# A planned kernel of four graph layers: a longer time in the plan for the transfers that sum the scores

## The chip, the cores and the metric

The kernel runs on one core of one Trainium2 chip. The metric is the device time of one execution in microseconds (us). Before the change it is 1678.89 us, the median of three runs (1675.96 to 1679.08).

A core has four engines that compute: TensorE (PE in the profile; PEld is its loading of weights), VectorE (DVE), ScalarE (ACT) and GpSimd (POOL). SyncE (SP) issues most of the transfers. Each engine takes its own instructions in the order in which the program lists them, and waits at an instruction until what it needs is there.

## What is computed

The input is 32 graphs of 512 nodes with 128 features each, and one adjacency matrix of 512 x 512 for all of them. Four layers follow each other; each normalises the features, applies a ReLU and adds its result to x. The change concerns layer 0, whose core is

```python
x_h = elu(h @ Wi + bi)
a_src = x_h @ We[:H, 0]
a_tgt = x_h @ We[H:, 0]
e = sigmoid(a_tgt[:, :, None] + a_src[:, None, :] + be[0])
e = e * (adj + ALPHA * (adj == 0))
agg = e @ x_h
self_part = x_h * sum(e, axis=-1)
recv = elu(concat(agg, self_part) @ Wn + bn)
out = concat(recv, x_h) @ Wm + bm
```

Layer 1 is a gated recurrent step, done five times, with two products by the adjacency in the reference (here both with the same matrix, so the kernel computes one). Layer 2 is one product by the adjacency and one by a weight. Layer 3 sums three powers of the adjacency.

## The kernel before

**Tiles.** One graph's features are a tile of 128 partitions x 512 elements, float32, 256 KB. Everything is done in such tiles: there are 36 of the kind `f` for features and scores, 4 of the kind `q` for float32r parts, 8 PSUM banks (`b`), 8 pieces of device memory (`m`) for tiles that are turned, and some small kinds. Float32r values are the short form[...]; a float32 tile is split in a high and a low part where the exact sum is wanted.

**The order of the work.** The kernel is written as a list of operations. Each has an engine, a time that the engine is taken (`us`), a due time, the values it reads and writes, and a `result`: the time from the end of its issue until its result can be used. A planner (class `Plan`, method `order`) goes through this list with a clock of its own: when an engine is free, it gives it the ready operation with the smallest due time, takes tiles as they come free by that clock, and writes the operations down. That sequence is the program. The figures `us` and `result` so decide only which instruction stands ahead of which in each engine's order, and which tile it gets[...]. The planner works in two stretches: the first 18 us of its clock, with small idle matmuls (L301) where TensorE has nothing to do, and the rest. The rest is planned twice, for an adjacency that float32r holds exactly and for one that it does not; these inputs take the first.

**The graphs.** The due times are set per graph: `begin(b)` for layer 0, 14 us apart for the first four graphs, then 56 us apart, and 30 us for the last four. Layer 1 follows 42 us after `begin` for graphs 0 to 3 and 112 us after it for most others. Several graphs are in different layers at once, so that TensorE has the products of one while the other engines work on another. Layers 0 to 2 are listed graph by graph, and layer 3 for four graphs together.

**Layer 0 around the change** (`layer0`). For each graph ScalarE (L620, tanh) and VectorE (L623) make four tiles of scores, `es[0]` to `es[3]`. They go two ways. TensorE multiplies them with the messages (L631) into the bank `pn`. And they are summed over all 512 source nodes: for graphs 0 and 1 by four products with ones; for the 30 others the four tiles are first added by transfers. SyncE copies `es[0]` to a tile `sums` (L641), and GpSimd issues three transfers, each of which adds one more tile to it (L644). Each writes the tile that the one before has written, so each waits for it. Then ScalarE rounds the sum to its high part (L648), VectorE makes the low part (L649), TensorE totals both over the partitions with a matrix of ones (L654), VectorE multiplies x_h by the total (L657), and TensorE adds that product with Wn (L442, helper `product`) to `pn`. An elu and the last product with Wm (L667) end the layer.

**Other names in the profile.** L442 is the helper of all float32 products (u3T, w4T, w3T, w5T and u5T are the weights of layer 1, Wi and Wn those of layer 0). L821 is layer 1's and 2's product by the adjacency, L902 and L911 are layer 3's, and L884 is layer 2's weight. L846, L447 and L853 are VectorE, ScalarE and VectorE of the gate between w4T and u5T. Lines L383 to L420 turn a tile by way of device memory, `m<-f` and `f<-m`. L479 is a small operation of GpSimd in each layernorm.

Of the kernel before, what the change touches and what calls it, by code (L numbers as in the profile page):

```python
# [41 lines left out]
class Plan:  # L42
# [16 lines left out]
    def op(self, eng, us, due, emit, reads=(), writes=(), two=None, keep=0, result=None,  # L59
           earliest=0.0):  # L60

        two = eng == "POOL" if two is None else two
        o = Op(eng, us, self.RESULT[eng] if result is None else result, emit, two, keep)
        o.earliest = earliest
        for v in reads:
            o.before.add(v.writer)
        for v in writes:  # L70
            o.before.update(v.readers)
            if v.writer:
                o.before.add(v.writer)
            elif v.kind and v.slot is None:
                o.takes.append(v)
        for v in reads:
            v.readers.append(o)
        for v in writes:
            v.writer, v.readers = o, []
        o.vals = [v.whole or v for v in dict.fromkeys([*reads, *writes])]  # L80
        for v in o.vals:
            v.left += 1
        for v in [*reads, *writes, *o.vals]:
            self.vals[v] = True
        o.before -= {o, None}
        o.due = max([due, *(b.due for b in o.before)])
        for b in o.before:
            b.after.append(o)
        self.ops.append(o)
# [124 lines left out]
def tile_four_graph_layers(  # L214
# [63 lines left out]
    def at(v):  # L278
        if v.tile is not None:
            return v.tile  # L280
        return places[v.kind][v.slot] if v.whole is None else at(v.whole)[:, v.part]
# [152 lines left out]
    def product(w, src, due, dst=None, start=True, stop=True, blocks=False):  # L434

        dst = dst or Val("b")
        def emit():
            to, of = at(dst), at(src)
            if blocks:
                to = to.rearrange("p (c q i) -> p q c i", c=NC, i=32)  # L440
                of = of.rearrange("p (q c i) -> p q c i", c=NC, i=32)
            nc.tensor.matmul(to, at(w), of, start=start, stop=stop)  # L442
        op("PE", T_MM, due, emit, [src, w], [dst])
        return dst
# [104 lines left out]
    def layer0(b, h, due):  # L549
# [85 lines left out]
        if b < 2:  # L635
            ps = Val("b")
            for jc in range(NC):
                product(ones, es[jc], d, ps, start=jc == 0, stop=jc == NC - 1)
        else:
            sums = [Val("f")]  # L640
            op("SP", T_DMA, d - 10, lambda: nc.sync.dma_start(at(sums[0]), at(es[0])),  # L641
               [es[0]], [sums[0]], result=2.6)
            for e in es[1:]:
                op("POOL", 1.0, d - 10, lambda e=e: nc.gpsimd.dma_start(  # L644
                    at(sums[0]), at(e), accum_op=ALU.add), [e, sums[0]], [sums[0]],
                   two=False, result=3.0)
            high, low, ps = Val("q"), Val("q"), Val("b")
            op("ACT", T_COPY, d, lambda: nc.scalar.copy(at(high), at(sums[0])), [sums[0]], [high])  # L648
            op("DVE", T_VEC, d, lambda: nc.vector.tensor_tensor(  # L649
                at(low), at(sums[0]), at(high).bitcast(F32), op=ALU.subtract),  # L650
                [sums[0], high], [low], two=True)
            def total():
                for n, part in enumerate((low, high)):
                    nc.tensor.matmul(at(ps), at(ones_r), at(part), start=n == 0, stop=n == 1)  # L654
            op("PE", 2 * T_PASS, d, total, [high, low, ones_r], [ps])
# [23 lines left out]
    def first_layer(b):  # L679
        h = layernorm(b, begin(b))  # L680
        layer0(b, h, begin(b))
# [316 lines left out]
```

## Time and profile before

| | us |
|---|---|
| median of three runs | 1678.89 |
| the profiled execution's own time | 1678.16 |
| its span, from the first instruction to the last | 1676.4 |
| TensorE busy | 1662.9 |
| VectorE busy | 1420.3 |
| ScalarE busy | 1130.5 |
| GpSimd busy | 239.6 |

The profile shows one execution. Busy time is the time in which an engine has an instruction under way; ends of matmuls are modelled, so that TensorE's busy time says little on whether it could be faster. "Idle before" is the time that an engine stood still just ahead of an instruction, with the one that released it. The clock granted to TensorE was full (0.999) throughout. The 90 adding transfers carry 23.6 MB in all and take 8.5% of the time of the 16 DMA engines; all others together take about a third.

### The profile page before, as it was taken

The page shows a single profiled execution, that of the slowest core. Times are in us where ns is not written, and L with a number is a line of the kernel's source. Part 1 is how long each engine was busy: PE and PEld are TensorE (multiplying, and loading weights), DVE is VectorE, ACT ScalarE, POOL GpSimd, SP SyncE. Part 2 cuts the span into 40 slices and gives each one's busy share as a digit, 9 for nine tenths or more (in the row PEclk, how much of TensorE's full clock was granted, in tenths as well). Part 3 has the DMA queues.
Part 4 walks back from the last instruction along what each step waited for, and adds up shares of the span by engine and source line. Part 5 has one row for each costly group of instructions (what it writes and reads, how often), then busy time and mean ns, then how long its engine had stood idle before and what let it go on. Part 6 is the DMA issues. An engine that isn't in the chain of part 4 may idle for free.

```text
span 1676.4 us, 21509 instructions
## 1 busy us (share of the span) xinstructions
PE 1662.9 (99%) x6615; PEld 1073.7 (64%) x6615; DVE 1420.3 (85%) x3327; ACT 1130.5 (67%) x2145; POOL 239.6 (14%) x243
## 2 busy tenths in 40 slices
PE   9999999999999999999999999999999999999998
PEld 7555555556666666666666666666666666666797
DVE  6888999999988888889888898888999988877742
ACT  8877677876875676656676676665777767655541
POOL 2311101211111111111101111111121110000110
PEclk9999999999999999999999999999999999999999
DMA  3444424444445434444434444344554543222301
GB/s 108 114 107 138 134 88 138 121 130 115 134 113 138 120 96 127 110 122 131 121 106 111 130 127 127 107 123 109 135 138 122 138 111 103 88 64 88 93 10 53
DMA packets 284157, 188.05 MB, mean 112 GB/s; under 512 B 77312, under 2 KB 236928, under 8 KB 284032
## 3 DMA queue, kind: packets, MB, share of 16 engines
q1 hardware_dynamic: 271072, 162.98, 32.5%
q0 software_dynamic: 12960, 23.60, 8.5%
q8 instruction: 54, 0.88, 0.2%
q14 instruction: 71, 0.58, 0.1%
HBM read 82.25 MB, written 72.81 MB: 92 GB/s over the span
## 4 chain that ended last, share of the span: by engine, by line
PE 62%; DMA 2%; DVE 1%; ACT 0%; issue 0%; SPq 0%; DVEq 0%; POOLq 0%
PE b L442 27%; PE b L821 13%; PE b L911 9%; PE b L902 5%; PE b L631 3%; PE b L667 2%; PE b L884 1%; DMA f<-f 1%; PE b L568 1%; DMA m<-f 1%; PE b L654 1%; DMA f<-m 0%; DVE f L383 0%; SPq L420 0%; ACT f L620 0%
## 5 line engine op out<-in xcount | busy, mean ns | idle before, releaser
L821 PE MATMUL b<-AQ,r 128*128 128x512 f32 x1024 | 303.8, 439 | 0.0
L431 ACT COPY f<-b 128x512 f32<-128x512 f32 x360 | 207.9, 586 | 120.6 <-PE b L821 87.2
L479 POOL TENSOR_TENSOR s<-s,nhalf 128x4 f32<-128x4 f32 x128 | 154.8, 1212 | 822.0 <-DVE s L477 702.6
L821 PEld LDWEIGHTS b<-AQ,r 128*128 128x128 f32 x1024 | 192.3, 188 | 89.3 <-issue 51.5
L846 DVE TENSOR_TENSOR f<-f,b 128x512 f32<-128x512 f32 x320 | 210.9, 676 | 26.6 <-PE b L442 26.2
L911 PE MATMUL b<-r,A_r 128*128 128x512 f32 x768 | 225.0, 427 | 0.0
L383 DVE STREAM_TRANSPOSE f<-f 128x512 f32<-128x512 f32 x244 | 204.7, 843 | 21.2 <-ACT f L487 20.4
L487 ACT ACTIVATE f<-x,s 128x128 f32<-128x128 f32 x512 | 210.5, 490 | 17.4 <-DVE s L482 16.9
L447 ACT ACTIVATE f<-f,b4w 128x512 f32<-128x512 f32 x160 | 115.4, 723 | 144.1 <-DVE f L846 143.5
L911 PEld LDWEIGHTS b<-r,A_r 128*128 128x128 f32 x768 | 139.0, 189 | 46.2 <-issue 24.4
L442 PE MATMUL b<-f,u5T 128*128 128x512 f32 x320 | 163.3, 593 | 1.0 <-DVE f L853 1.0
L442 PE MATMUL b<-f,u3T 128*128 128x512 f32 x320 | 163.3, 593 | 1.0 <-DMA f<-m 1.0
L442 PE MATMUL b<-f,w4T 128*128 128x512 f32 x320 | 162.8, 592 | 0.0
L442 PE MATMUL b<-f,w3T 128*128 128x512 f32 x320 | 162.4, 592 | 0.0
L442 PE MATMUL b<-f,w5T 128*128 128x512 f32 x320 | 162.4, 592 | 0.0
L644 POOL DMA_DIRECT2D f<-f x90 | 80.7, 896 | 536.4 <-DVE f L865 58.1
L821 PE MATMUL b<-A_r,r 128*128 128x512 f32 x512 | 151.9, 438 | 0.0
L863 DVE TENSOR_TENSOR f<-f,f 128x512 f32<-128x512 f32 x160 | 109.2, 683 | 48.9 <-ACT f L447 48.4
L902 PEld LDWEIGHTS b<-V,f 128*128 128x128 f32 x1024 | 131.4, 191 | 25.6 <-issue 19.9
L447 ACT ACTIVATE f<-b,b5w 128x512 f32<-128x512 f32 x160 | 109.4, 684 | 56.0 <-PE b L442 53.5
L447 ACT ACTIVATE f<-f,b3w 128x512 f32<-128x512 f32 x160 | 114.9, 719 | 43.1 <-DVE f L846 42.2
L795 DVE TENSOR_TENSOR r<-f,r 128x512 fp32r<-128x512 f32 x192 | 130.5, 682 | 12.6 <-ACT r L791 12.4
(106 smaller groups left out, 2539.3 us busy)
## 6 DMA issues: line engine op xcount, KB each, us to landing
m<-f SPq DMA_DIRECT2D x244, 256.0 KB, 2.1
f<-m SPq DMA_DIRECT2D x184, 256.0 KB, 2.9
f<-f POOLq DMA_DIRECT2D x90, 256.0 KB, 3.6
f<-m SPq DMA_DIRECT2D x240, 64.0 KB, 2.4
x<-in_x_dram SPq DMA_DIRECT2D x32, 256.0 KB, 3.2
out_dram<-x SPq DMA_DIRECT2D x32, 256.0 KB, 2.5
f<-f SPq DMA_DIRECT2D x30, 256.0 KB, 2.3
f<-d SPq DMA_DIRECT2D x28, 256.0 KB, 5.1
```

Of the source, the lines that this page charges most:

```text
L383: op("DVE", us, due, lambda: nc.vector.transpose(view_out(at(blocks)), view_in(at(src))), [src], [blocks])
L431: op("ACT", us, due, lambda: nc.scalar.copy(at(t), at(src)), [src], [t])
L442: nc.tensor.matmul(to, at(w), of, start=start, stop=stop)
L447: op("ACT", us, due, lambda: nc.scalar.activation(at(dst), at(src), AF.Tanh, bias=at(bias), scale=scale), [src, bias], [dst])
L479: op("POOL", 1.35, due, lambda: nc.gpsimd.tensor_tensor(stat(SCALE), stat(VAR), at(neg_half), op=ALU.pow), [s, neg_half], [s])
L487: nc.scalar.activation(at(h)[:, ts(c, P)], at(X[b])[:, c, :], AF.Relu, bias=stat(SHIFT)[:, c : c + 1], scale=stat(SCALE)[:, c : c + 1],)
L795: op("DVE", T_VEC, due, lambda: nc.vector.tensor_tensor(part(lo), whole(), part(hi).bitcast(F32), op=ALU.subtract), [src, hi], [lo], two=two)
L821: nc.tensor.matmul(at(pa), at(part)[:, ts(jc, P)], view(at(columns)[:, jc, :]), start=jc == n == 0, stop=jc == NC - 1 and n == PARTS - 1,)
L846: op("DVE", T_VEC, d, lambda: nc.vector.tensor_tensor(at(s), at(u), at(pg), op=ALU.add), [u, pg], [s])
L863: op("DVE", T_VEC, d, lambda c=c, h=h: nc.vector.tensor_tensor(at(c), at(c), at(h), op=ALU.subtract), [c, h], [c], two=True)
L902: nc.tensor.matmul(at(pz)[:, ts(i, D)], at(hT[i])[:, ts(ic, P)], at(V[k]), start=i == 0, stop=last and i == G - 1,)
L911: nc.tensor.matmul(at(pz), at(adjT)[:, jc, ts(ic, P)], at(part), start=False, stop=jc == NC - 1 and n == PARTS - 1,)
```

## The change

The planner's time from the end of the issue of an adding transfer to its result is longer; nothing else is touched.

```diff
             for e in es[1:]:
                 op("POOL", 1.0, d - 10, lambda e=e: nc.gpsimd.dma_start(
                     at(sums[0]), at(e), accum_op=ALU.add), [e, sums[0]], [sums[0]],
-                   two=False, result=3.0)
+                   two=False, result=4.6)
```

`op` takes the engine, the issue's time and the due time[...]. The planner now lists what depends on the sum, the next add first of all, as ready 1.6 us later after each add. The instructions are the same ones; their order and their tiles are the planner's.

## The prediction

> **What bounds the kernel now.** I read the page first, then the chain that ended last, then the waits, and last the timeline around the matmul that sums the scores.
>
> The page: the span, the engines, and the chain that ended last by engine.
>
> ```profile
> span 1676.4 us, 21509 instructions
> ...
> PE 1662.9 (99%) x6615; PEld 1073.7 (64%) x6615; DVE 1420.3 (85%) x3327; ACT 1130.5 (67%) x2145; POOL 239.6 (14%) x243
> ...
> PE 62%; DMA 2%; DVE 1%; ACT 0%; issue 0%; SPq 0%; DVEq 0%; POOLq 0%
> ```
>
> TensorE is busy nearly always, and what else is on the chain is small. But a busy TensorE may be a waiting one, so I take its true need from unbroken stretches of the chain (start us, duration us, what):
>
> ```profile
> 853.33 4.29 PE b L442 x10
> ...
> 1539.12 3.65 PE b L821 x16
> ...
> 1618.46 5.36 PE b L902 x48
> ```
>
> That is 0.429 us for each matmul of a float32 product, 0.228 for a float32r pass of 512 columns, 0.112 for one of 128 columns. By count: 2000 (L442, L631) x 0.429 = 858; 2368 float32r passes (L821, L911, L654, L809) x 0.228 = 540; 2154 narrow ones (L902, L667, L568, L884, the idle L301) x 0.112 = 241; 93 small ones about 9. Sum 1648 of the 1670 us until the last matmul ends; 6.4 us of subtractions and stores follow it. The 22 us between are: 1.0 before the first matmul, some 7 us spread over the float32r passes (0.231 instead of 0.228 apiece), and 13.4 us of true stalls, found as start-to-start intervals longer than the price of the matmul. No reordering can gain more than these 13.4 us, 0.8%. Whom TensorE waits for (us in total, times, longest), by recorded ends:
>
> ```profile
> PE b L654 <- DVE q L649: 2.8, 5, 0.9
> PE b L301 <- DVE ones L296: 1.0, 1, 1.0
> PE b L442 <- DVE f L853: 1.0, 2, 0.6
> PE b L442 <- DMA f<-m: 1.0, 1, 1.0
> PE b L631 <- DVE f L623: 0.6, 1, 0.6
> PE b L442 <- DVE f L657: 0.5, 2, 0.3
> ```
>
> The first is the matmul that totals the scores (L654); the last is the product right after it (Wn, behind L657). By start-to-start intervals L654 lost 3.7 us in 6 stalls, and 0.7 in the matmul behind it (after each stall the second matmul starts 0.1 late too); Wn 1.1 and 0.5. Together 6.0 us on the path to the total. The reason stands in the waits of the engines before it:
>
> ```profile
> ACT q L648 <- DMA f<-f: 29.9, 19, 4.9
> ...
> DVE q L649 <- ACT q L648: 16.3, 13, 2.6
> ```
>
> In 19 of 30 graphs ScalarE reaches the copy of the sum before the last adding transfer has landed and stands there, and VectorE behind it. The timeline shows the worst case:
>
> ```profile
> 636.09 0.86 POOL L644 DMA_DIRECT2D f<-f  x1 [3.20 <-ACT f L431]
> ...
> 639.43 0.62 ACT L648 CAST q<-f 128x512 fp32r<-128x512 f32 x1 [2.62 <-DMA f<-f]
> 640.09 0.69 DVE L649 TENSOR_TENSOR q<-f,q 128x512 fp32r<-128x512 f32 x1 [2.09 <-ACT q L648]
> ...
> 640.83 0.73 PE L654 MATMUL b<-q,ones_r 128*128 128x512 f32 x2 [0.87 <-DVE q L649]
> ...
> 643.22 1.12 PE L442 MATMUL b<-f,Wn_sb 128*128 128x512 f32 x2 [0.28 <-DVE f L657]
> ```
>
> The transfers themselves (line L644: ns min/median/max; us from issue to landing):
>
> ```profile
> L644 POOL DMA_DIRECT2D f<-f x90: 850/917/1097, 49.5 to 1380.6; - x90
> ...
> DMA to landing us min/median/max: 3.2/3.6/4.9
> ```
>
> [...] each of the three starts some 0.53 us after the landing of the last. [...] here 3.6 from issue, 0.9 of it issuing. [...]
>
> **The change part by part.** It adds no instruction and removes none; the planner's time from the end of an adding issue to its result goes from 3.0 to 4.6 us, so that three adds count 3 x 5.6 = 16.8 us instead of 3 x 4.0 = 12.0. Measured they take 3.6 + 0.53 = 4.1 us apiece, 12.8 us (median; 11.2 to 14.2) from the first issue to the copy. The old figure was short in the mean by under 1 us and in the worst case by 2; the new one is generous by 2.6 to 5.6.
>
> What this does to the order I take from the two built programs. The first 59.7 us of TensorE's work and the last 274.6 us (351 entries of the list) stand in the same order. Between, 965 of the list's 1892 TensorE entries change place, by 1.5 places in the mean over all and 19 at most. Between a graph's first add and its total stand, in the issue order, 14.3 us of TensorE work before (median; 13.2 to 19.2) and 19.4 after (17.5 to 21.9). What is needed in the trace from the first add's start to L654 in the five cases with a large stall: 14.8, 15.2, 12.9, 14.0, 14.8 us, against 13.2, 15.0, 13.2, 15.4, 14.1 of work then and 17.5, 19.3, 20.1, 20.3, 18.5 after. So all five have 2.7 us or more to spare, and the other graphs too. Term one: the 6.0 us go; at least the 3.3 of the recorded ends, at most 6.0. I take 6.0, since each Wn stall but the one at 67 us follows a late total.
>
> What moves later: the total, VectorE's product (L657), Wn, the elu behind it and the add to x, by 5 us per graph. In the steady state layer 1 of the graph begins only 2 x 56 us after layer 0, which is due to end after 44, so nothing waits. The scores, the sums and a PSUM bank (pn) are held 5 us longer; TensorE has no stall for a bank in this trace above 0.1 us, and the planner keeps 12 tiles free of layer 0. I cost that at nothing; without that cover it is one product (0.9 us) per late bank. ScalarE and VectorE get back 29.9 and 16.3 us of standing, worth nothing by themselves since TensorE is the bound. On GpSimd the small power operations (L479) of the layernorms stand among the adds of one sum 33 times instead of 27, and fewer adds should hold them up (12 waits of 48.0 us for a landing before).
>
> What gets tighter elsewhere: I summed the rows of each path from one matmul over other engines to the next and compared with the TensorE work that covers it. Paths through SyncE transfers with under 4 us to spare, the total left out: 7 before, 9 after. Gate to product u5T with a cover below 3.6 us: 6 before, 8 after. These kinds of path cost 3.2 us of stalls in the reordered stretch before. Term two: a third more, +1.1, and +0.4 for graphs 2 and 3, where two covers are 0.1 us short after the change; from 0 to +5, -3.2 if they vanish. Sum: -6.0 + 1.5 = -4.5 us on a profiled time of 1678.2 (span 1676.4). The median of the three runs is 1678.9, 0.7 above; so 1674.4.
>
> **The rivals.** A: the gain is eaten by new stalls of the other kinds. The list is tight, every stretch of TensorE is full, and ScalarE's and VectorE's orders change over 1300 us. For it: the counts above rise. Against: they rise by few. With +4 new, -2.0 us: 1677. B: the other stalls of the stretch go as well, being accidents of one order: -6.0 - 3.2 = -9.2, 1669.7. Nothing speaks for it but chance. C, the other side: the start. Graphs 2 and 3 are the first with adding transfers, and for them layer 1 is due 42 us after layer 0 begins, with layer 0 due to end after 44: here the 4.8 us lie on a path. GpSimd's order also puts the first add of graph 4 ahead of the third of graph 3, so a late graph 4 holds graph 3. Between 60 and 130 us TensorE must then find other work; if it finds none, two graphs x 4.8 us. That makes the kernel slower by over 3.4 us only if it costs more than 6.0 + 3.4 = 9.4, and 9.6 is its whole price: 1682.5. Against: the worked-out covers there are short by 0.1 us alone.
>
> **How the numbers follow.** 0.2%, 3.4 us, is about what a measurement of this kernel can tell from no change. The forecast (3.4 to 6.5 us faster) 0.45, B 0.15, A (within 3.4 us) 0.30, C 0.10. Faster 0.60, same 0.30, slower 0.10. The range runs from B's 1670 to 1681.5, short of most of C; it takes in the -9.2 of all stalls gone and +2.6 of new ones beyond the gain. The forecast alone: 1672 to 1675.5.
>
> **What would show it.** ScalarE's waits of L648 for the transfer fall from 29.9 us to under 5, VectorE's of L649 from 16.3 to under 3; the row of L654 waiting for L649 leaves TensorE's waits; time from the first add to L654 grows to some 18 us; TensorE's stalls fall from 13.4 to about 9. I am wrong if L654 still waits, if TensorE's busy time between 60 and 130 us drops, or if waits for L853 or f<-m grow by more than 3 us.

## The result, and the profile after

The changed kernel takes 1674.93 us (median of 20 runs, 1674.01 to 1675.9), the kernel before 1677.45 us in the runs beside it (20 runs, 1675.94 to 1680.67). The ratio is 0.9981 with a 95% interval of 0.9975 to 0.9987: 0.19% faster, some 3 us (2.5 by the two medians), and by the bound of 0.2% just on the side of no change. The forecast was 4.5 us. The kernel before was itself 1.4 us faster in these 20 runs than in the three shown ahead.

The page of the changed kernel: span, engines, and the chain that ended last.

```profile
span 1673.7 us, 21484 instructions
...
PE 1661.3 (99%) x6615; PEld 1076.9 (64%) x6615; DVE 1422.1 (85%) x3327; ACT 1135.0 (68%) x2145; POOL 238.2 (14%) x243
...
PE 97%; DVE 2%; ACT 0%; issue 0%; DVEq 0%
```

The span fell by 2.7 us. TensorE's waits (us in total, times, longest) read quite unlike those of before:

```profile
PE b L821 <- DVE r L795: 3.2, 1, 3.2
PE b L631 <- DVE f L623: 1.3, 2, 0.7
PE b L301 <- DVE ones L296: 1.0, 1, 1.0
PE b L442 <- DVE f L853: 0.5, 1, 0.5
```

The total (L654) and the product behind it (Wn) are gone from the list. In their place stands one wait of 3.2 us, for the low part of a tile of layer 1 (L795). ScalarE's row for the copy of the sum (line L648: durations; then what its engine waited for, and who waited for it) has no wait left:

```profile
L648 ACT CAST q<-f x30: 601/618/634, 68.4 to 1385.5; 128x512 fp32r<-128x512 f32 x30
its engine sat idle before it (us, times) until:
who waited for it (us, times):
  DVE q L649: 8.5, 10
```

From the last landing to this copy pass 3.9 us now (median), where it was 0.02. VectorE still waits 8.5 us for the copy, since the plan puts its low part right behind it; no matmul waits for that.

The wait of 3.2 us, in the timeline (start us, us, engine, line):

```profile
319.76 0.38 SPq L396 DMA_DIRECT2D f<-m  x1
...
321.12 1.88 PE L442 MATMUL b<-f,u3T 128*128 128x512 f32 x4
...
321.55 3.18 ACT L487 ACTIVATE f<-x,s 128x128 f32<-128x128 f32 x8
...
324.63 0.61 ACT L791 CAST r<-f 128x512 fp32r<-128x512 f32 x1
...
325.43 0.69 DVE L795 TENSOR_TENSOR r<-f,r 128x512 fp32r<-128x512 f32 x1
...
326.18 3.09 PE L821 MATMUL b<-AQ,r 128*128 128x512 f32 x8 [3.17 <-DVE r L795]
```

The turned tile is issued by SyncE at 319.76 us and these transfers land 2.9 us later (median of that line there), at some 322.7; ScalarE takes it at 324.63, behind two normalisations. TensorE has nothing else in its order, and stands. The chain of this stretch runs through VectorE alone for the 21 us before it. The same place by stretches of time (engine busy us with instruction counts, the granted clock, DMA), first of the changed kernel:

```profile
core 0: us, PE busy (x) PEld busy (x) DVE busy (x) ACT busy (x) POOL busy (x), PEclk, DMA share, GB/s
310.00:320.00 10.00, 10.00 (x32) 5.85 (x31) 9.97 (x21) 6.95 (x14) 2.78 (x3) 1.00 0.70 144
320.00:325.00 5.00, 3.01 (x13) 1.46 (x11) 4.90 (x11) 5.00 (x13) 0.00 (x0) 1.00 0.41 135
325.00:330.00 5.00, 3.82 (x10) 2.67 (x11) 4.87 (x13) 5.00 (x12) 1.41 (x1) 0.70 0.63 147
330.00:335.00 5.00, 5.00 (x17) 3.08 (x16) 4.32 (x7) 3.71 (x7) 0.00 (x0) 0.95 0.60 193
```

and of the kernel before:

```profile
310.00:320.00 10.00, 10.00 (x38) 6.25 (x37) 10.00 (x19) 10.00 (x23) 2.97 (x3) 1.00 0.69 144
320.00:325.00 5.00, 4.40 (x16) 2.67 (x15) 3.78 (x7) 3.38 (x8) 0.00 (x0) 1.00 0.74 197
325.00:330.00 5.00, 4.55 (x17) 2.22 (x15) 5.00 (x9) 2.61 (x5) 0.00 (x0) 1.00 0.59 147
```

VectorE is full in both up to 320 us. But ScalarE, full in the old order, is busy 6.95 of 10 us in the new one, then jammed for ten. And behind TensorE's 3.2 us of idleness the granted clock falls. The 0.70 is a mean over five microseconds; cut where the clock changes, the changed kernel shows half the clock for 3.41 us and the full one on both sides:

```profile
325.00:327.05 2.05, 0.87 (x4) 0.73 (x5) 1.92 (x9) 2.05 (x6) 1.41 (x1) 1.00 0.61 183
327.05:330.46 3.41, 3.41 (x8) 2.20 (x7) 3.27 (x5) 3.41 (x8) 0.00 (x0) 0.50 0.71 159
330.46:335.00 4.54, 4.54 (x16) 2.82 (x15) 4.00 (x6) 3.25 (x6) 0.00 (x0) 1.00 0.56 173
```

The matmuls after the stall start 0.1 to 0.4 us late apiece, 1.8 us together, as half the clock for 3.41 us would have it. So this place costs 3.3 + 1.8 = 5.1 us.

Stalls by the same start-to-start intervals as in the prediction add up for both kernels, in us:

| | before | after |
|---|---|---|
| ahead of 60 us | 3.6 | 3.7 |
| 60 to 130 us, other than the total | 0.7 | 2.0 |
| the total and Wn | 6.0 | 0.0 |
| 315 to 345 us, other than the total | 1.3 | 5.1 |
| elsewhere | 1.8 | 0.3 |
| sum | 13.4 | 11.1 |

### The profile page after: what moved, and what is told of

Read it like the earlier page. It is cut to its first block, busy times and chain, and to the rows that moved or that the text cites. A ratio compares the mean times of both kernels' runs of the same rounds, so it can differ in the third digit from the quotient of the medians.

```text
span 1673.7 us, 21484 instructions
## 1 busy us (share of the span) xinstructions
PE 1661.3 (99%) x6615; PEld 1076.9 (64%) x6615; DVE 1422.1 (85%) x3327; ACT 1135.0 (68%) x2145; POOL 238.2 (14%) x243
## 4 chain that ended last, share of the span: by engine, by line
PE 97%; DVE 2%; ACT 0%; issue 0%; DVEq 0%
PE b L442 44%; PE b L821 21%; PE b L911 11%; PE b L902 7%; PE b L631 6%; PE b L667 3%; PE b L568 2%; PE b L884 2%; PE b L301 1%; PE b L654 1%; DVE s L474 0%; PE b L371 0%; DVE f L383 0%; DVE f L623 0%; DVE r L795 0%; DVE f L846 0%
## 5 line engine op out<-in xcount | busy, mean ns | idle before, releaser
L821 PE MATMUL b<-AQ,r 128*128 128x512 f32 x1024 | 303.8, 439 | 3.2 <-DVE r L795 3.2
L821 PEld LDWEIGHTS b<-AQ,r 128*128 128x128 f32 x1024 | 192.5, 189 | 92.3 <-issue 49.5
L487 ACT ACTIVATE f<-x,s 128x128 f32<-128x128 f32 x512 | 210.3, 488 | 25.9 <-DVE s L482 25.5
L821 PE MATMUL b<-A_r,r 128*128 128x512 f32 x512 | 150.6, 436 | 0.0
L795 DVE TENSOR_TENSOR r<-f,r 128x512 fp32r<-128x512 f32 x192 | 130.1, 680 | 15.0 <-ACT r L791 14.8
```

Of the source, the lines that this page charges most:

```text
L487: nc.scalar.activation(at(h)[:, ts(c, P)], at(X[b])[:, c, :], AF.Relu, bias=stat(SHIFT)[:, c : c + 1], scale=stat(SCALE)[:, c : c + 1],)
L795: op("DVE", T_VEC, due, lambda: nc.vector.tensor_tensor(part(lo), whole(), part(hi).bitcast(F32), op=ALU.subtract), [src, hi], [lo], two=two)
L821: nc.tensor.matmul(at(pa), at(part)[:, ts(jc, P)], view(at(columns)[:, jc, :]), start=jc == n == 0, stop=jc == NC - 1 and n == PARTS - 1,)
```

## The experiments

### Less to wait for, in both orders

The third add of each graph is not issued, though the plan still counts it; so a quarter of the scores is left out of the total. Applied to the kernel before and to the changed one, this moves no instruction.

```diff
-                op("POOL", 1.0, d - 10, lambda e=e: nc.gpsimd.dma_start(
+                op("POOL", 1.0, d - 10, lambda e=e: None if e is es[3] else nc.gpsimd.dma_start(
```

> The order of the kernel before, with the third adding transfer of each graph left out (three of the four score tiles are summed; the plan still counts it). Nothing else moves, so the sum is there some 4.1 us sooner. If the waits for the sum cost what the start-to-start intervals say, 6.0 us go, and perhaps the 2.0 us of stalls that follow them at 330 and 633 us: ratio to before 0.995 to 0.997. If the time comes back in other stalls, 0.9985 or more.

Measured: 1671.17 us, ratio 0.9954 (0.9940 to 0.9967), 7.6 us less than the 1678.77 us of before beside it. The stalls fell from 13.4 to 6.4 us, those of the total and Wn from 6.0 to 0.5. VectorE's wait for the copy, in the waits of this run:

```profile
DVE q L649 <- ACT q L648: 0.9, 2, 0.7
```

The old order, with the sum there in time, is faster than the changed kernel. So the waits for the sum were worth what the intervals said and a little more, and the new order gave some of it back.

> The changed order with the third adding transfer left out in the same way. If the changed order has taken every wait for the sum off TensorE's path, this gives nothing: as the changed kernel, 0.998 of before, within 1 us. If some of them were still hidden in other rows, it is faster than the changed kernel by 2 us or more: 0.997 or less.

Measured: 1674.36 us, ratio 0.9972 (0.9963 to 0.9982); its interval overlaps that of the changed kernel. The stall of 3.3 us stands in the same place (324.8 us), the mean clock is 0.998 in this profile as in that of the changed kernel, and the stalls sum to 9.7 us. The changed order has no wait for the sum left to remove; what fell is 0.8 us between 60 and 130 us, and some 0.6 ahead of it. This also answers a rival reading of the run before, that 30 transfers fewer are worth the 7.6 us by themselves: here the same 30 are gone, for next to nothing.

### More to wait for, in both orders

The third adding transfer is issued twice, so that the total counts one tile twice.

```diff
-                op("POOL", 1.0, d - 10, lambda e=e: nc.gpsimd.dma_start(
-                    at(sums[0]), at(e), accum_op=ALU.add), [e, sums[0]], [sums[0]],
+                op("POOL", 1.0, d - 10, lambda e=e: [nc.gpsimd.dma_start(
+                    at(sums[0]), at(e), accum_op=ALU.add) for _ in range(2 if e is es[3] else 1)],
+                   [e, sums[0]], [sums[0]],
```

> The order of the kernel before, with the third tile added twice (a fourth transfer, so the sum is there some 4.1 us later; the total counts one tile twice). From the first add to the total 14.3 us of TensorE work stand against then some 18 us needed: about 3 us for each of 30 graphs, +60 to +110 us, ratio 1.035 to 1.065. If TensorE's cover doesn't decide, +10 us at most, 1.006.

Measured: 1806.79 us, ratio 1.0763 (1.0735 to 1.0791): 128 us more, above the expected range. The edit adds a line, so that L648, L649 and L654 are L649, L650 and L655 in these two kernels. Its waits:

```profile
ACT q L649 <- DMA f<-f: 147.1, 30, 8.9
DVE q L650 <- ACT q L649: 116.1, 28, 6.6
...
PE b L655 <- DVE q L650: 80.6, 27, 5.4
```

The 27 stalls at the total are what was expected, 3 us apiece. What I left out is the clock: its mean in this profile is 0.973, which on 1648 us of matmuls is an estimated 45 us. (It is 0.96 in each of the first two stretches of 400 us, and 0.98 from 800 to 1200 and from 1200 to 1680 us.)

> The changed order with the third tile added twice. 19.4 us of work stand against some 18 us needed; after the changed kernel's third landing the copy comes 3.9 us later in the mean, so about half the graphs are late, by 20 us in all on ScalarE and some 10 on TensorE: ratio to before 1.000 to 1.008. If the longer figure only shuffled the order, this costs as much as the same addition to the order before: 1.03 or more.

Measured: 1692.10 us, ratio 1.0085 (1.0070 to 1.0101), some 17 us above the changed kernel; a little over the expected range. Its waits:

```profile
DVE q L650 <- ACT q L649: 26.8, 17, 5.1
ACT q L649 <- DMA f<-f: 24.0, 13, 6.0
...
PE b L655 <- DVE q L650: 4.1, 5, 1.8
```

Here 13 graphs are late instead of 30, and TensorE stalls five times at the total instead of 27. The same added transfer costs 128 us in one order and some 17 in the other. That is the longer figure at work: it buys cover of about one transfer per graph. It would have been worth far more had the transfers been slower; with the real ones, the old cover was short by little.

### Other figures

```diff
-                   two=False, result=4.6)
+                   two=False, result=3.8)
```

and 3.4, 4.2 and 5.2 in the same way.

> The same plan with 3.4 instead of 4.6. The adds are planned at 4.4 us each, measured 4.1: waits of L648 for the transfer around 10 us, of TensorE for the total around 1. Time 0.996 to 1.000, by what the new order does elsewhere. If the gain of 4.6 were an accident of that order, the waits of L648 say nothing on the time here.

> The same plan with 3.8: adds planned at 4.8 us each. Waits of L648 under 4 us, TensorE's for the total under 0.5; time 0.996 to 0.999, the scatter being other stalls of the order.

> The same plan with 4.2: adds planned at 5.2 us each. Waits of L648 under 1 us, none of TensorE for the total; time 0.995 to 0.999. With neither the waits for the sum nor a stall as at 326 us, as the order before with two adds: 0.9955.

> 5.2 for all: adds planned at 6.2 us each. No waits for the sum, as with 4.6; holding the scores and the bank 1.8 us longer costs nothing. 0.995 to 0.9995 by what the order has at 320 to 335 us. If the longer hold costs, slower than before.

The figure for a part of the graphs alone:

```diff
-                   two=False, result=4.6)
+                   two=False, result=4.6 if b >= G else 3.0)
```

and, for graphs 2 and 3 alone, `4.6 if b < G else 3.0`.

> 4.6 for graphs 4 to 31 alone, 3.0 for graphs 2 and 3. If the start is where the change loses, this is faster than the changed kernel (0.995 to 0.997). If the loss sits at 320 to 335 us, the time goes with what this order has there: without a stall 0.9955, with one as in the changed kernel 0.998. Waits of L648 for the transfer near 0 after graph 3.

> 4.6 for graphs 2 and 3 alone. Nearly all waits for the sum stay (L648 over 20 us, TensorE's stalls at the total 3 to 6 us), so it isn't faster than before by more than 0.1%, and slower if the start costs: 0.999 to 1.003.

Measured, in the order of the figure; stalls by start-to-start intervals in each profile, in us:

| figure | median us | ratio to before (95%) | waits of L648 for the sum | stalls at the total and Wn | other stalls 315 to 345 us | all stalls | span |
|---|---|---|---|---|---|---|---|
| 3.0 (before) | 1677.45 | 1 | 29.9 | 6.0 | 1.3 | 13.4 | 1676.4 |
| 3.4 | 1679.00 | 0.9999 (0.9990 to 1.0008) | 10.9 | 2.3 | 6.5 | 14.8 | 1677.6 |
| 3.8 | 1671.11 | 0.9955 (0.9940 to 0.9971) | 10.0 | 0.7 | 0.0 | 7.1 | 1669.8 |
| 4.2 | 1676.58 | 0.9988 (0.9980 to 0.9997) | 0.2 | 1.2 | 2.4 | 12.0 | 1674.8 |
| 4.6 (the change) | 1674.93 | 0.9981 (0.9975 to 0.9987) | 0.0 | 0.0 | 5.1 | 11.1 | 1673.7 |
| 5.2 | 1676.52 | 0.9979 (0.9972 to 0.9987) | 0.0 | 1.9 | 2.2 | 11.5 | 1674.1 |
| 4.6, graphs 4 to 31 | 1671.37 | 0.9951 (0.9935 to 0.9966) | 0.2 | 0.6 | 0.3 | 6.5 | 1669.3 |
| 4.6, graphs 2 and 3 | 1681.23 | 1.0007 (0.9995 to 1.0018) | 31.5 | 6.8 | 0.3 | 14.2 | 1677.0 |

The ratios compare, the medians across rows don't: the kernel before took 1677.45 us beside 4.6, 1678.33 beside 3.4, 3.8 and 4.2, and 1680.73 beside the last three. The kernel of the last row ran from 1676.06 to 1690.02 us; its profile is of a run of 1678.82.

Three readings. First, in all eight the span less the stalls is 1662.6 to 1663.0 us: the stalls are the whole difference between these profiled executions. Second, the waits of ScalarE follow the figure as they should, but they aren't the time: 3.8 has 10 us of them (I had expected under 4, and 0.996 at best) and is among the fastest, since TensorE's stalls at the total are down to 0.7. The adds need 4.1 us, 3.8 plans 4.8. Third, most of what is beyond that is decided by what each order happens to do at 315 to 345 us, and less of it between 60 and 130. 3.4 saves 3.7 us at the total and pays 5.2 at this one place. Its windows:

```profile
320.00:325.00 5.00, 4.87 (x16) 2.66 (x15) 5.00 (x9) 5.00 (x14) 0.00 (x0) 1.00 0.33 111
325.00:330.00 5.00, 1.12 (x2) 0.30 (x2) 4.95 (x14) 5.00 (x12) 1.00 (x1) 0.78 0.84 241
330.00:335.00 5.00, 4.70 (x17) 3.66 (x18) 3.29 (x6) 4.49 (x9) 0.39 (x1) 0.53 0.81 222
```

TensorE is busy for 1.1 of 5 us, ScalarE and VectorE are full, and the clock goes to 0.53. With 3.8 the same stretch has no gap, and ScalarE was full in the ten microseconds ahead of it, as in the kernel before:

```profile
310.00:320.00 10.00, 10.00 (x35) 5.67 (x34) 9.01 (x18) 9.96 (x23) 2.82 (x3) 1.00 0.76 153
320.00:325.00 5.00, 5.00 (x17) 2.78 (x16) 5.00 (x9) 5.00 (x11) 0.00 (x0) 1.00 0.61 181
325.00:330.00 5.00, 5.00 (x18) 3.13 (x17) 4.97 (x10) 4.00 (x8) 0.00 (x0) 1.00 0.67 186
```

The eight orders agree in this. ScalarE is busy for 10.00, 9.96, 9.88 and 8.78 us of the ten before 320 us in the kernel before, 3.8, and the parts from graph 4 on and for graphs 2 and 3, whose other stalls are 1.3 us at most; and for 7.95, 7.35, 6.95 and 5.83 us with 4.2, 5.2, 4.6 and 3.4, whose other stalls are 2.2 to 6.5. Work that ScalarE has not done by 320 us crowds it afterwards. That this is the cause is a reading of eight profiles; no run here changes it alone.

The graphs from 4 on carry the gain: with them alone the kernel is as fast as with 3.8. Graphs 2 and 3 alone bring none. The longer hold of scores and bank shows no price, 5.2 being as fast as 4.6. At the start the profiles can be paired, since TensorE's orders are the same up to 88 us in the kernel before and the part from graph 4 on, and up to 114 us in the changed kernel and the part for graphs 2 and 3. Stalls other than the total from 60 to 130 us are 0.7 us in both of the first pair and 2.0 in both of the second. So the longer figure for graphs 2 and 3 costs 1.3 us there, and takes away some 0.8 of stalls at the total and Wn.

### The one place, by hand

In the changed order two entries were moved ahead of what ScalarE and VectorE do before them.

```diff
-            issue(plan.order())
+            order = plan.order()
+            if exact:
+                for o, ahead in ((1070, 1826), (1071, 1253)):
+                    o, ahead = plan.ops[o], plan.ops[ahead]
+                    order.remove(o)
+                    order.insert(order.index(ahead), o)
+            issue(order)
```

1070 and 1071 are the high and the low part for the matmul at 326.18 us, 1826 is a normalisation (L487), 1253 a gate operation of layer 1 (L865).

> The changed order with two entries moved: ScalarE's high part and VectorE's low part for the product by the adjacency that starts at 326.18 us go ahead of one normalisation on ScalarE (L487) and of a gate operation and statistics on VectorE (L865, L474, L476, L477). If VectorE's and ScalarE's crowded queues make the 3.3 us stall there, it falls to some 1.7 us, the clock no longer drops behind it (1.7 us more), and the kernel is 1.6 to 3.4 us faster than the changed one: ratio to before 0.996 to 0.9972. If the stall is of the data (the turn by way of device memory), it stays: 0.998.

Measured: 1673.46 us, ratio 0.9973 (0.9961 to 0.9984); span 1671.3. The edit adds lines, so that L821, L791 and L795 are L827, L797 and L801 in these two kernels. TensorE's two matmuls in the timeline:

```profile
323.71 2.11 PE L827 MATMUL b<-AQ,r 128*128 128x512 f32 x8 [1.48 <-DVE r L801]
...
327.08 1.12 PE L442 MATMUL b<-f,w4T 128*128 128x512 f32 x2 [1.25 <-ACT f L431]
```

The stall is halved as expected, and the clock stays at 1.00; but most of the other half comes up again 3.4 us later, at a copy behind the same normalisation, and the ratio is just outside of what I expected (0.996 to 0.9972). The next run moves that as well.

```diff
-                for o, ahead in ((1070, 1826), (1071, 1253)):
+                for o, ahead in ((1070, 1826), (1573, 1826), (1071, 1253), (1999, 2152)):
```

> As the run with two entries moved, and two more: ScalarE's copy (L431) for which TensorE waited 1.5 us at 327 us goes ahead of the same normalisation, and VectorE's low part of the sum (L649) ahead of two transposes (L383). If the stall of this place is one of ScalarE's crowded queue, the 1.5 us go too: ratio to before 0.9955 to 0.9968, near the order before with two adds (0.9954). If the place has too little work ready whatever stands first, the stall comes up at the next matmul: 0.9973.

Measured: 1674.94 us, ratio 0.9967 (0.9958 to 0.9977), not to be told from the run before it; span 1672.7. The first of TensorE's waits:

```profile
PE b L827 <- DVE r L801: 3.0, 2, 1.6
```

The ratio alone would fit the stalls' being gone; the profile says otherwise. The copy's stall is gone and 3.0 us stand in two waits for low parts. So within these few entries the three microseconds don't go away, they go to the next matmul. That fits a place with too little ready for TensorE, whatever stands first; that every other move would fail too is not shown. That the clock no longer falls is what both moves gained at most; the intervals touch that of the changed kernel, so the times alone don't show even that.

## Why the prediction was right, and where it was off

**The sum as a whole.** Forecast -6.0 + 1.5 = -4.5 us, measured -6.0 + 3.7 = -2.3 in stalls and -2.7 in span. That 1674.93 us stands beside the forecast 1674.4 is in part luck, because the kernel before was 1.4 us faster beside it. The gain that I held for the likeliest, 3.4 to 6.5 us, did not come; a smaller one did.

**The bound and the price of the stalls.** Right: spans differ by the stalls alone, to 0.4 us over eight orders.

**Term one, the 6.0 us of the total and Wn.** Right: they are 0.0 after the change, and taking the wait away in the old order gave 7.6 us, the 6.0 with some that follow from them. The cover worked out from the order held: from the first add to the total pass 20.1 us now (median), 15.2 before, and no graph is late. It is no exact measure: in two of the five cases shown the work listed before the change was already more than the time taken (13.2 us against 12.9, 15.4 against 14.0), and TensorE stalled all the same, so it was some way into that work when the add started. The margins were wide enough for this not to matter. That one more transfer costs 128 us in the old order and some 17 in the new shows that it is this cover, and not chance, that removed them.

**Term two, +1.5 us of new stalls.** The mechanism was right and the size was off: it measures +3.7 (60 to 130 us +1.3, the place at 315 to 345 us +3.8, elsewhere -1.5, ahead of 60 us +0.1). The step that failed is "a third more": I counted the paths with little to spare, 7 before and 9 after, and priced one more path as the mean of the old ones. A stall has no mean price. One path of this kind, of layer 1 through SyncE (the record doesn't show whether it is among the nine), gave 3.3 us. ScalarE and VectorE were both crowded when it came, which a sum of durations along a path doesn't see; moving its two parts ahead of that crowd took the stall from 3.17 to 1.48 us. And behind the idleness the clock fell to 0.50, which cost 1.8 us here and which I had not priced: the clock is nowhere in my sum. Behind shorter waits, 1.48 us in the changed order with two entries moved and 2.2 us with figure 4.2 (at 327 us), it stayed at 1.00.

**What was costed at nothing.** The longer hold: right, 5.2 costs no more than 4.6. ScalarE's freed time: right. VectorE's wait for the copy was to fall under 3 us and is 8.5, and GpSimd's waits at an add for a landing were to be fewer and went from 12 (48.0 us) to 14 (62.2 us): wrong, and harmless.

**The rivals.** A, a gain partly eaten by other stalls, is the nearest: 3 us by the ratio lies within its bound of 3.4. B, all other stalls gone too, did not come with 4.6, but 3.8 and the part from graph 4 on came near it. C, the start, cost 1.3 us where 9.4 were needed; its sign came in small, TensorE being busy for 68.9 us from 60 to 130 us and not 69.4. TensorE's stalls were to fall to about 9 and fell to 11.1.

## What to carry to other kernels

Where a planner orders the work, a transfer that is planned too short leaves a wait at its reader, and the price can be read beforehand as start-to-start intervals on the engine that bounds the kernel. But a changed figure draws a whole new order: besides the wait that it removes, count on a scatter as large as the gain, and try several figures, because one bad place decides. Price the clock too: behind the gap of 3.2 us it cost 1.8 us more.

## What the runs showed of the hardware

The clock at the one place, with TensorE's waits there:

| kernel | TensorE's waits there, us | busy of 5 us, 325 to 330 | clock 320 to 325, 325 to 330, 330 to 335 us |
|---|---|---|---|
| before | longest 1.0 | 4.55 | 1.00, 1.00, 1.00 |
| figure 3.4 | 4.2 | 1.12 | 1.00, 0.78, 0.53 |
| figure 4.2 | 2.2 | 3.05 | 1.00, 1.00, 1.00 |
| 4.6 (the change) | 3.2 | 3.82 | 1.00, 0.70, 0.95 |
| the change, two entries moved | 1.5 and 1.3 | 3.75 | 1.00, 1.00, 1.00 |
| the change, four entries moved | two, 3.0 in all, longest 1.6 | 3.61 | 1.00, 1.00, 1.00 |

At half the clock, from 327.05 to 330.46 us in the changed kernel, float32r matmuls of 512 columns start 0.43 us apart, where they take 0.24 us just ahead of it and 0.23 behind it. How much idleness takes the clock down, these six places don't show.

The adding transfers take about as long in both orders: from issue to landing 3.6 us in the kernel before (median; 3.2 to 4.9) and 3.7 in the changed one (3.2 to 6.2).
